# Layer 3's softmax sums gathered by accumulating DMAs in a four-layer graph network, with layer 0's residual by DMA and a new order

## The chip, the core and the metric

The kernel runs on one core of a Trainium2 chip. The time is that of one execution on the device, in microseconds (us), given as the median of several runs. A profile is a record of one such execution, with each instruction's start and length on each engine: PE (matrix products), PEld (its weight loads), DVE (vector), ACT (scalar), POOL (general, also a DMA issuer) and SP (a DMA issuer). Sixteen DMA engines move data for all issuers.

## The reference

Sixteen graphs of 1024 nodes with 128 features go through four layers. Each layer's result is added to its input and normalised over the features. `adj` holds zeros and ones; about one in 32 is one.

```python
# layer 0: one head of 128; attention over the neighbours
e = leaky_relu(s[:, :, None] + t[:, None, :], 0.2)
H_out = relu(softmax(e + mask) @ H)
# layer 1: 8 heads of 16, the same form, then elu
# layer 2: mean over the neighbours, times a matrix, plus a linear part; layernorm, relu
# layer 3: 4 heads of 32
Wh = einsum('bsf,hfd->bhsd', x, W)
scores = einsum('bhsd,bhtd->bhst', Wh, Wh) / sqrt(32)
scores = where(adj > 0, scores, NEG_INF)
h = einsum('bhst,bhtd->bhsd', softmax(scores), Wh)
# after every layer: x = layernorm(x + layer(x))
```

## The kernel before

The nodes of a graph are eight blocks of 128 (NB), in two halves of four blocks or 512 columns (HALF). The mask is loaded once per graph, transposed, as eight tiles m of 128 x 1024 in one-byte floats: POOL issues these DMAs (L557), and they turn integers into floats on the way. The softmax weights are always held transposed: a block of 128 source nodes on the partitions, the target nodes along the free axis.

**Layers 0 and 1.** DVE makes a tile of weights in one instruction (L636 in layer 0, L788 in layer 1): the larger of a row R, spread over all partitions, and a number per partition q, times the mask. PE multiplies it with the features (L648, L796). The row R is computed as a small column tile, turned by PE, copied by ACT, stored to memory by SP and read back by SP spread over all partitions (L753, 512 KB each); eight such rows are needed per graph in layer 1, four per group of heads. The factors that go into q and R come after a maximum over all partitions, an instruction on POOL (L398). Layer 0's result is taken from the accumulator by ACT with a relu (L669), which also sums it, and DVE adds the layer's input x0 (L689), which SP loaded in its natural form (L624).

**Layer 2** is a block of 96 products per half on the mask itself (L928), between turning x (L366), a product with the weights (L375) and a layernorm.

**Layer 3** is worked by halves of the target nodes and, in each half, by the eight source blocks j. ACT makes `gap` from the mask (L1066). PE first puts a large negative number where an edge is missing (L1076), then adds the scores (L1087), for four heads, into two PSUM tiles `sc` of two banks each from the pool `wk`. ACT takes the exponential of each (L1123) into a tile z3 of two heads. PE then multiplies (L1102): for each of two pairs of heads a step with four products, two heads times (their features, and a tile of ones). The features' products give the numerator and those with ones the sum of the weights, 32 equal rows of it. So a block j takes two such steps, and two accumulators (`acc3`) hold both pairs. At a half's end ACT copies the accumulators (L1139), PE turns them, and DVE divides (L1150, L1153) and adds to x3 (L1164).

**The order of the work.** All steps are handed to a planner that runs while the program is built. Each step has an engine, an estimated time, a due time, the buffers that it reads and writes and a lag until its result can be used. The planner goes through time and gives each engine the step that can start earliest, the one with the earlier due time first. The program is then one fixed order of instructions on every engine and each waits, in that order, for what it needs. Two or more graphs are in work at a time: layer 1 of one beside layers 2 and 3 of the one before. `PERIOD` is the distance between the due times of graphs. Buffers come from pools of fixed size: `wk` two tiles of two banks, `acc1` and `acc3` two banks each, z3 four tiles, R seven, z nine. Everything that is turned by PE (L366, L480) also goes through `wk`, as do the products before each layer.

Of the kernel before, what the change touches and what calls it, by code (L numbers as in the profile page):

```python
# [20 lines left out]
F32 = mybir.dt.float32  # L21
# [7 lines left out]
P = 128  # L29
# [47 lines left out]
class Plan:  # L77
# [8 lines left out]
    SAME = 0.0  # L86
    URGENT = 61.2
    AHEAD = 4322.0
# [136 lines left out]
def tile_binary(  # L225
# [3 lines left out]
    xT_in: bass.AP,  # L229
    adjT: bass.AP,  # L230
# [35 lines left out]
    acc3s = [psum.tile([P, HALF], F32, name=f"acc3_{n}") for n in range(2)]  # L266
# [25 lines left out]
    LATER1 = -3.8  # L292
    LATER3 = 48.7
# [28 lines left out]
    plan.scarce = ("wk", "acc1", "acc3")  # L322
    plan.pool("wk", wks)
    plan.pool("acc1", acc1s)
    plan.pool("acc3", acc3s)
    places("m", 6 * HB, [P, N], F8)
    places("R", 7, [P, N])
    places("z", 9, [P, N])
    places("z3", 4, [P, 2, HALF])
    places("oT1", 1, [P, N])  # L330
    places("oT3", 1, [P, N])
    places("x0", 1, [P, NB, P])
# [53 lines left out]
    def turned(x_nat, chunk, due):  # L386

        pt, xT = Buf("wk", "pt"), Buf("xTc", "xTc")
        step(
            "PE", 0.44, due, lambda: transposes(pt.t, [x_nat.t[:, chunk * HB + k, :] for k in range(HB)]),  # L390
            [(x_nat, chunk), xT], [pt],
        )
        step("ACT", 0.47, due, lambda: nc.scalar.copy(xT.t, pt.t[:, :HALF]), [pt], [xT])
        return xT
# [80 lines left out]
    def rows_everywhere(r, flat, count, due):  # L475

        pt, rT = Buf("wk", "pt"), Buf("rT", "rT")
        kept = Buf(f"rows{int(count > 1)}", "rows")
        step(
            "PE", 0.2, due, lambda: nc.tensor.transpose(pt.t[: count * NB, :P], flat(r.t), ident), [r, rT], [pt]  # L480
        )
        step("ACT", 0.2, due, lambda: nc.scalar.copy(rT.t[: count * NB, :], pt.t[: count * NB, :P]), [pt], [rT])
        step(
            "SP", 0.5, due,
            lambda: nc.sync.dma_start(
                out=kept.t.rearrange("h (k p) -> (h k) p", p=P), in_=rT.t[: count * NB, :]
            ),
            [rT], [kept], lag=2.5,
        )
        return kept  # L490
# [60 lines left out]
    def before0(b, due):  # L551
        G = graphs[b]
        G["m"] = [Buf("m", f"m_{b}_{j}") for j in range(NB)]
        for j, m in enumerate(G["m"]):
            step(
                "POOL", 0.55, due - 60 + 5 * j,
                lambda m=m, j=j: nc.gpsimd.dma_start(out=m.t, in_=adjT[b, j * P : (j + 1) * P, :]),  # L557
                [], [m], lag=5.0, floor=12.0 + 3 * j if b == 1 else max(due - 60 + 5 * j, 0.0),
            )
        x0 = G["x"] = Buf("x0", f"x0_{b}")  # L560
# [63 lines left out]
        step("SP", 2.0, due, lambda: nc.sync.dma_start(out=x0.t, in_=natural(x[b])), [], [x0], lag=2.5)  # L624

    def layer0(b, due):
# [4 lines left out]
        for half in range(2):  # L631
# [32 lines left out]
            for n in range(2):  # L664
# [23 lines left out]
                "DVE", 0.6, at,  # L688
                lambda ks=ks: nc.vector.tensor_tensor(y.t[:, ks, :], y.t[:, ks, :], G["x"].t[:, ks, :], ALU.add),  # L689
                [G["x"]], [(y, half)],  # L690
# [87 lines left out]
    def layer1(b, due, span):  # L778
# [3 lines left out]
        for g in range(2):  # L782
# [39 lines left out]
            oT, pt, rd = Buf("oT1", "oT1"), Buf("wk", "pb1"), little("rd1", [P, NB, G1, 1])  # L822
# [31 lines left out]
    def last1(b, due):  # L854

        G = graphs[b]
        o, x1, e = G["x2"], G["x1"], Buf("oT1", "e")
        step(
            "ACT", 1.0, due, lambda: nc.scalar.activation(e.t, o.t.rearrange("p k f -> p (k f)"), AF.Exp), [o], [e]
        )  # L860
        step(
            "DVE", 1.26, due,
            lambda: nc.vector.scalar_tensor_tensor(o.t, in0=o.t, scalar=0.0, in1=x1.t, op0=ALU.max, op1=ALU.add),
            [x1], [o],
        )
        step(
            "DVE", 1.26, due,
            lambda: nc.vector.scalar_tensor_tensor(o.t, in0=blocks(e.t), scalar=1.0, in1=o.t, op0=ALU.min, op1=ALU.add),
            [e], [o],
        )  # L870
        tot = little("tot", [P, NB])
        for half in range(2):
            sums(o, half, tot, due)
        layernorm(o, tot, due + 3)
# [114 lines left out]
    def before3(b, due):  # L989
# [6 lines left out]
        for chunk in range(2):  # L996
            xT, ps = turned(x3, chunk, due + chunk), Buf("wk", "h3")
# [18 lines left out]
            pt = Buf("wk", "pt")  # L1016
# [14 lines left out]
        sq, norms, bound = Buf("oT3", "sq"), little("norms", [P, NB * H3]), little("bound", [P, 1])  # L1031
# [23 lines left out]
    def layer3(b, due, span):  # L1055
# [3 lines left out]
        for half in range(2):  # L1059
            cols = slice(half * HALF, (half + 1) * HALF)  # L1060
            av = [Buf("acc3", f"av3_{g}") for g in range(2)]
# [34 lines left out]
            def weighted(j, g, z, av=av):  # L1096

                for h in range(2):
                    at = D3 * (2 * g + h)
                    for n, lhsT in enumerate((hhs[j // HB].t[:, j % HB, at : at + D3], ones)):  # L1100
                        at = 64 * h + 32 * n
                        nc.tensor.matmul(  # L1102
                            av[g].t[at : at + 32, :],
                            lhsT=lhsT,
                            rhs=z.t[:, h, :],
                            start=j == 0,
                            stop=j == NB - 1,
                        )

            for j in range(NB):  # L1110
# [4 lines left out]
                step("ACT", 0.68, at - 8, lambda j=j, gap=gap, f=missing: f(j, gap), [m[j]], [gap])  # L1115
# [12 lines left out]
                for g in (0, 1):  # L1128
                    step(
                        "PE", 0.87, at + LATER3, lambda j=j, g=g, z=zs[g], f=weighted: f(j, g, z),  # L1130
                        [zs[g], hhs[j // HB]], [av[g]], mode="32 columns",
                    )
            at = due + span * (half + 1) / 2
            oT, pt, rd = Buf("oT3", "oT3"), Buf("wk", "pb3"), little("rd3", [P, 2 * HB, 2, 1])
            o = Buf("rest", "o3")
            for g in range(2):
                step(
                    "ACT", 0.48, at,
                    lambda g=g, oT=oT, av=av: nc.scalar.copy(oT.t[:, g * HALF : (g + 1) * HALF], av[g].t),  # L1139
                    [av[g]], [(oT, g)],  # L1140
# [7 lines left out]
            def share(pt=pt, rd=rd, o=o):  # L1148
                pn = blocks(pt.t).rearrange("p m (c w) -> p m c w", c=2)
                nc.vector.reciprocal(rd.t, pn[:, :, :, D3 : D3 + 1])  # L1150
                for g in range(2):
                    of_g = slice(g * HB, (g + 1) * HB)
                    nc.vector.tensor_tensor(  # L1153
                        o.t.rearrange("p k (h d) -> p k h d", h=H3)[:, :, 2 * g : 2 * g + 2, :],
                        pn[:, of_g, :, :D3],
                        rd.t[:, of_g].to_broadcast([P, HB, 2, D3]),
                        ALU.mult,
                    )

            step("DVE", 1.07, at, share, [pt], [rd, o])  # L1160
# [22 lines left out]
    PERIOD = 129.0  # L1183
    weights(-198)
    for b in range(B):
        at = b * PERIOD
        at0 = 25 if b == 1 else at
        before0(b, at0 - 50)
        layer0(b, at0)
        before1(b, at + 25)  # L1190
        layer1(b, at + 99, 111)
        last1(b, at + 165)
        layer2(b, at + 165)
        before3(b, at + 223)
        layer3(b, at + 321, 108)
# [579 lines left out]
def tile_adj_resnorm(ctx: ExitStack, tc: tile.TileContext, x, adjT, *weights_and_out, xT):  # L1775
# [3 lines left out]
    tile_binary(tc, x, xT, adjT, *weights_and_out, wrong)  # L1779
# [44 lines left out]
```

## Time and profile before

| | |
|---|---|
| time, median of 3 runs | 2258.46 us (2258.31 to 2259.9) |
| the profiled execution, span from first to last instruction | 2254.1 us |
| PE busy | 2074.9 us, 92% of the span |
| DVE busy | 1902.1 us, 84% |
| ACT busy | 1743.5 us, 77% |
| POOL busy | 130.9 us, 6% |
| DMA moved | 119.86 MB, mean 53 GB/s |
| mean granted PE clock | 0.980 |

The profile gives no other time for the profiled execution than its span; the median of the runs lies 4.4 us above it. A line of a group names the line of the code, the engine, the operation, what it writes and reads, how often, then the time it was busy and the mean of one instruction in ns, and last how long its engine was idle just before and for whom it waited. In the 40 slices of the span each digit is a busy share in tenths. A busy PE isn't PE at its peak.

### The profile page before, as it was taken

How to read it: one execution, taken by the hardware profiler on the slowest of the kernel's cores; microseconds unless marked ns; L12 is line 12 of the kernel's file. 1: busy time of each engine (PE TensorE's matmuls, PEld its weight loads, DVE VectorE, ACT ScalarE, POOL GpSimd, SP SyncE). 2: the span in 40 equal slices, each digit the busy share in tenths (PEclk: the TensorE clock that was granted, in tenths of full speed). 3: DMA queues.
4: the chain of work that ended last, by engine and by line, in shares of the span. 5: the costliest groups of instructions: out<-in, count | busy, mean ns of one | idle time of the engine just before them, and what ended most of it. 6: DMA issues, size and time to landing. Idle time of an engine off the chain costs nothing.

```text
span 2254.1 us, 55458 instructions
## 1 busy us (share of the span) xinstructions
PE 2074.9 (92%) x23472; PEld 971.1 (43%) x23472; DVE 1902.1 (84%) x2854; ACT 1743.5 (77%) x4376; POOL 130.9 (6%) x187
## 2 busy tenths in 40 slices
PE   4857999999999999999999999999999999998876
PEld 4613545353534544363544535353454436242311
DVE  2899999989989989999999998998999999997211
ACT  3413769878787879878787987878787987868786
POOL 1010000100000000000000010000000000000000
PEclk9878999999999999999999999999999999999999
DMA  6122130312323040222314031232304122200000
GB/s 97 59 77 36 37 85 18 92 38 77 48 86 48 20 100 25 86 39 86 48 32 99 18 91 38 77 48 85 50 20 96 29 77 39 77 11 11 2 11 12
DMA packets 80851, 119.86 MB, mean 53 GB/s; under 512 B 7384, under 2 KB 58704, under 8 KB 80592
## 3 DMA queue, kind: packets, MB, share of 16 engines
q1 hardware_dynamic: 62160, 99.43, 13.1%
q0 software_dynamic: 18432, 16.79, 9.0%
q8 instruction: 186, 3.05, 0.6%
q14 instruction: 73, 0.60, 0.1%
HBM read 157.55 MB, written 8.97 MB: 74 GB/s over the span
## 4 chain that ended last, share of the span: by engine, by line
PE 52%; DVE 24%; ACT 20%; issue 3%; DMA 1%; POOL 0%; DVEq 0%; POOLq 0%; ACTq 0%
DVE z L788 18%; PE acc L648 10%; PE acc L1102 9%; PE acc L796 9%; PE wk L928 8%; ACT z L1123 6%; PE wk L1087 6%; PE wk L366 4%; ACT junk L430 4%; ACT x L468 3%; PE wk L375 3%; ACT gap L1066 3%; PE wk L1076 2%; PE wk L1001 1%; ACT hd L620 1%
## 5 line engine op out<-in xcount | busy, mean ns | idle before, releaser
L788 DVE SCALAR_TENSOR_TENSOR z<-R,q,m 128x1024 f32<-128x1024 f32 x1024 | 1248.9, 1279 | 16.1 <-PE acc L796 8.3
L1123 ACT ACTIVATE z<-wk,low 128x1024 f32<-128x1024 f32 x512 | 545.3, 1105 | 58.2 <-PE wk L1087 56.7
L796 PE MATMUL acc<-z,hh 128*32 128x512 f32 x4096 | 512.3, 612 | 46.1 <-DVE z L788 44.6
L1102 PE MATMUL acc<-z,hh 128*32 128x512 f32 x2048 | 516.2, 604 | 33.4 <-ACT z L1123 33.4
L1102 PE MATMUL acc<-z,ones 128*32 128x512 f32 x2048 | 516.1, 604 | 0.0
L430 ACT ACTIVATE junk<-x,off 128x128 f32<-128x128 f32 x640 | 256.2, 400 | 230.8 <-DVE off L424 214.6
L1087 PE MATMUL wk<-whT,turn 32*64 32x512 f32 x4096 | 286.3, 615 | 0.0
L468 ACT ACTIVATE x<-x,shift,rstd 128x128 f32<-128x128 f32 x640 | 259.3, 485 | 7.7 <-DVE shift L462 7.6
L648 PEld LDWEIGHTS acc<-hd,z 128*128 128x128 f32 x2048 | 237.3, 193 | 34.8 <-ACT x L669 12.6
L796 PEld LDWEIGHTS acc<-z,hh 128*32 128x32 f32 x4096 | 110.6, 110 | 326.8 <-issue 194.6
L648 PE MATMUL acc<-hd,z 128*128 128x129 f32 x2048 | 244.7, 278 | 5.9 <-DVE z L636 4.5
L1102 PEld LDWEIGHTS acc<-z,hh 128*32 128x32 f32 x2048 | 97.9, 109 | 279.1 <-issue 190.2
L928 PE MATMUL wk<-y,m 128*128 128x128 bf16 (+1 forms) x3072 | 182.9, 220 | 24.5 <-ACT z L1123 19.9
L1066 ACT ACTIVATE gap<-m,neg_one 128x512 bf16<-128x512 fp8e5 x256 | 183.4, 718 | 20.6 <-DMA m<-in_adj_dram 20.6
L928 PEld LDWEIGHTS <-m 128*128 128x128 fp8e5 x3072 | 181.0, 98 | 37.0 <-issue 27.3
L636 DVE SCALAR_TENSOR_TENSOR z<-R,q,m 128x512 f32<-128x512 f32 x240 | 162.8, 746 | 1.0 <-DMA R<-rows 1.0
L1102 PEld LDWEIGHTS acc<-z,ones 128*32 128x32 f32 x2048 | 97.6, 109 | 83.0 <-issue 83.0
L1076 PEld LDWEIGHTS <-far 32*32 32x32 bf16 x4096 | 35.7, 88 | 210.0 <-issue 198.2
L430 ACT ACTIVATION_READ_ACCUMULATOR junk<-x,off 128x1 f32 x640 | 120.4, 188 | 0.0
L1076 PE MATMUL wk<-gap,far 32*32 32x512 bf16 x4096 | 113.3, 386 | 3.4 <-DVE rest L1153 1.7
L557 POOL DMA_DIRECT2D m<-in_adj_dram x128 | 68.3, 540 | 796.2 <-ACT gap L1066 765.8
L1087 PEld LDWEIGHTS wk<-whT,turn 32*64 32x64 f32 x4096 | 59.8, 130 | 58.6 <-issue 58.6
(119 smaller groups left out, 1859.7 us busy)
## 6 DMA issues: line engine op xcount, KB each, us to landing
R<-rows SPq DMA_DIRECT2D x139, 512.0 KB
m<-in_adj_dram POOLq DMA_DIRECT2D x128, 128.0 KB, 5.6
xT<-in_xT_dram SPq DMA_DIRECT2D x32, 256.0 KB
x<-in_x_dram SPq DMA_DIRECT2D x16, 512.0 KB
out_dram<-x SPq DMA_DIRECT2D x15, 512.0 KB
rows<-rT SPq DMA_DIRECT2D x16, 32.0 KB
out_dram<-x SPq DMA_DIRECT2D x2, 256.0 KB
z<-in_L_gnn_a_dram SPq DMA_DIRECT2D x2, 128.0 KB
```

Source lines behind the costliest of these rows:

```text
L430: nc.scalar.activation(junk.t, y.t[:, k, :], AF.Square, bias=off.t[:, k : k + 1], accum_out=squared.t[:, k : k + 1])
L468: nc.scalar.activation(y.t[:, k, :], y.t[:, k, :], AF.Identity, bias=shift.t[:, k : k + 1], scale=rstd.t[:, k : k + 1])
L636: nc.vector.scalar_tensor_tensor(z.t[:, (j % 2) * HALF : (j % 2 + 1) * HALF], in0=R0.t[:, cols], scalar=q.t[:, j : j + 1], in1=m[j].t[:, c ...
L648: nc.tensor.matmul(av[k // 2].t.rearrange("p (k c) -> p k c", k=2)[:, k % 2, : P + 1], lhsT=z.t[:, at : at + P], rhs=hd.t[:, j, : P + 1], ...
L788: nc.vector.scalar_tensor_tensor(z.t, in0=G["R"][h].t, scalar=q.t[:, j, h : h + 1], in1=m[j].t, op0=ALU.max, op1=ALU.mult)
L796: nc.tensor.matmul(av[half].t[32 * c : 32 * c + 32, :], lhsT=hh.t[:, j, at : at + 32], rhs=zs[c].t[:, half * HALF : (half + 1) * HALF], st ...
L928: nc.tensor.matmul(ps.t[:, k * SLOT : k * SLOT + part.stop - part.start], lhsT=m[j].t[:, rows_i], rhs=y2.t[:, j, part], start=j == 0 and n ...
L1066: nc.scalar.activation(gap.t, m[j].t[:, cols], AF.Square, bias=neg_one, accum_out=squares[:, at : at + 1], saturate=False)
L1076: nc.tensor.matmul(sc[h // 2].t[c * 32 : (c + 1) * 32, (h % 2) * HALF : (h % 2 + 1) * HALF], lhsT=far[rows_r, rows_r], rhs=gap.t[rows_r, : ...
L1087: nc.tensor.matmul(sc[h // 2].t[r * 64 : (r + 1) * 64, (h % 2) * HALF : (h % 2 + 1) * HALF], lhsT=turns[j // HB].t[rows_h, j % HB * P + r ...
L1102: nc.tensor.matmul(av[g].t[at : at + 32, :], lhsT=lhsT, rhs=z.t[:, h, :], start=j == 0, stop=j == NB - 1,)
L1123: lambda g=g, sc=sc, zs=zs: nc.scalar.activation(zs[g].t.rearrange("p h n -> p (h n)"), sc[g].t, AF.Exp, bias=low.t, scale=S3),
```

## The change

In layer 3 the products with the tile of ones are no longer made for each block. A block's step on PE is now one set of four products, one for each head, into a single accumulator `av`. The exponentials of a half are added up in memory: the z3 tiles of the first block stay in place, and for each of the seven later blocks POOL issues two DMAs, one for each z3 tile, that add the tile (512 KB) onto that of the first block. When the last has landed, one set of four products with ones gives the sums of the weights for all four heads, into a bank of the new pool `one`. The planner counts 0.55 us for the issue of such a DMA and a lag of 5.0 (`SUMMED`).

In layer 0, DVE's addition of the input is replaced by two DMAs per graph, issued on POOL, that add x (given a second time by the host as `x_rows`, laid out by partition) onto y. The load of x0 on SP and its tile go.

Of the accumulators `acc3` one bank becomes the pool `one`, through which turned rows and layer 3's products before the scores now go in place of `wk`. z3 has six tiles in place of four; the three tiles oT1, oT3 and the two uses beside them share one tile `wide`. Due times, spacings and the planner's constants are new, so the order of the instructions on all engines is another.

```diff
-    SAME = 0.0
-    URGENT = 61.2
-    AHEAD = 4322.0
+    SAME = 0
+    URGENT = 63.35
+    AHEAD = 4322
...
-    acc3s = [psum.tile([P, HALF], F32, name=f"acc3_{n}") for n in range(2)]
+    acc3s = [psum.tile([P, HALF], F32, name="acc3_0")]
+    ones_psum = [psum.tile([P, HALF], F32, name="one_0")]
...
-    LATER1 = -3.8
-    LATER3 = 48.7
+    LATER1 = -5.84
+    LATER3 = 75.02
+    SUMMED = 5.0
...
-    places("z3", 4, [P, 2, HALF])
-    places("oT1", 1, [P, N])
-    places("oT3", 1, [P, N])
-    places("x0", 1, [P, NB, P])
+    places("z3", 6, [P, 2, HALF])
+    places("wide", 1, [P, N])
...
-        pt, xT = Buf("wk", "pt"), Buf("xTc", "xTc")
+        pt, xT = Buf("one", "pt"), Buf("xTc", "xTc")
...
-        pt, rT = Buf("wk", "pt"), Buf("rT", "rT")
+        pt, rT = Buf("one", "pt"), Buf("rT", "rT")
...
-        step("SP", 2.0, due, lambda: nc.sync.dma_start(out=x0.t, in_=natural(x[b])), [], [x0], lag=2.5)
...
             step(
-                "DVE", 0.6, at,
-                lambda ks=ks: nc.vector.tensor_tensor(y.t[:, ks, :], y.t[:, ks, :], G["x"].t[:, ks, :], ALU.add),
-                [G["x"]], [(y, half)],
+                "POOL", 0.55, at,
+                lambda ks=ks: nc.gpsimd.dma_start(out=y.t[:, ks, :], in_=x_rows[b, :, ks, :], accum_op=ALU.add),
+                [], [(y, half)], lag=SUMMED,
             )
...
-            xT, ps = turned(x3, chunk, due + chunk), Buf("wk", "h3")
+            xT, ps = turned(x3, chunk, due + chunk), Buf("one", "h3")
...
-            av = [Buf("acc3", f"av3_{g}") for g in range(2)]
+            av, weights_sum = Buf("acc3", "av3"), Buf("one", "sum3")
...
+            def weighted(j, zs, av=av):
+
+                for h in range(H3):
+                    nc.tensor.matmul(
+                        av.t[32 * h : 32 * h + 32, :],
+                        lhsT=hhs[j // HB].t[:, j % HB, h * D3 : (h + 1) * D3],
+                        rhs=zs[h // 2].t[:, h % 2, :],
+                        start=j == 0,
+                        stop=j == NB - 1,
+                    )
+
+            def totals(zs, into):
+
+                for h in range(H3):
+                    nc.tensor.matmul(
+                        into.t[32 * h : 32 * h + 32, :], lhsT=ones, rhs=zs[h // 2].t[:, h % 2, :], start=True, stop=True
+                    )
+
+            def added(z, into):
+                nc.gpsimd.dma_start(out=into.t, in_=z.t, accum_op=ALU.add)
...
-                for g in (0, 1):
+                step(
+                    "PE", 0.87, at + LATER3, lambda j=j, zs=zs, f=weighted: f(j, zs),
+                    [*zs, hhs[j // HB]], [av], mode="32 columns",
+                )
+                first = first or zs
+                for g in (0, 1) if j else ():
                     step(
-                        "PE", 0.87, at + LATER3, lambda j=j, g=g, z=zs[g], f=weighted: f(j, g, z),
-                        [zs[g], hhs[j // HB]], [av[g]], mode="32 columns",
+                        "POOL", 0.55, at + LATER3, lambda z=zs[g], into=first[g], f=added: f(z, into),
+                        [zs[g]], [first[g]], lag=SUMMED,
                     )
+            step(
+                "PE", 0.87, at + LATER3, lambda zs=first, into=weights_sum, f=totals: f(zs, into),
+                first, [weights_sum], mode="32 columns",
+            )
...
-    PERIOD = 129.0
-    weights(-198)
+    PERIOD = 123.89
+    weights(-160.44)
     for b in range(B):
         at = b * PERIOD
         at0 = 25 if b == 1 else at
-        before0(b, at0 - 50)
+        before0(b, at0 - 48.02)
         layer0(b, at0)
-        before1(b, at + 25)
-        layer1(b, at + 99, 111)
-        last1(b, at + 165)
-        layer2(b, at + 165)
-        before3(b, at + 223)
-        layer3(b, at + 321, 108)
+        before1(b, at + 9.06)
+        layer1(b, at + 95.36, 120.08)
+        last1(b, at + 154.67)
+        layer2(b, at + 147.85)
+        before3(b, at + 211.97)
+        layer3(b, at + 309.2, 104.17)
```

## The prediction

> **What bounds the kernel now.** I read first the page's busy shares and its 40 slices, then the steady stretch by windows, the chain, the groups, and last the DMA views.
>
> ```profile
> PE 2074.9 (92%) x23472; PEld 971.1 (43%) x23472; DVE 1902.1 (84%) x2854; ACT 1743.5 (77%) x4376; POOL 130.9 (6%) x187
> ...
> PE   4857999999999999999999999999999999998876
> ...
> DVE  2899999989989989999999998998999999997211
> ...
> DMA  6122130312323040222314031232304122200000
> ```
>
> PE and DVE are both near 9 tenths from slice 8 to slice 36, and the DMA engines at 2 to 3. So the share over the span hides a close race. The chain repeats itself: layer 2's block of products comes every 128.8 us (1220.11 - 1091.33, 1348.89 - 1220.11, and so on from 318.20 to 1864.22). Windows cut at these points give one period, one graph's worth of work:
>
> ```profile
> 446.99:575.79 128.80, 126.29 (x1462) 59.42 (x1462) 118.46 (x178) 108.17 (x274) 8.36 (x11) 1.00 0.24 59
> 1220.11:1348.89 128.78, 126.27 (x1462) 59.42 (x1462) 118.55 (x178) 108.16 (x274) 8.36 (x11) 1.00 0.26 59
> ```
>
> The columns are length, then busy PE, PEld, DVE, ACT, POOL, the granted clock, the DMA share, GB/s. PE works 126.3 of 128.8 us at clock 1.00: PE is the bound. DVE works 118.5 and idles 10.3, ACT 108.2, the DMA engines 0.25 x 128.8 = 32 us. The chain's PE stretches show the price of a weighting step of layer 3: 24 products in 2.58 us, so eight in 0.86.
>
> ```profile
> 1220.11 11.30 PE wk L928 x192
> ...
> 1284.93 2.58 PE acc L1102 x24
> ...
> 1348.89 11.30 PE wk L928 x192
> ```
>
> ```profile
> L1102 PE MATMUL acc<-z,hh 128*32 128x512 f32 x2048 | 516.2, 604 | 33.4 <-ACT z L1123 33.4
> L1102 PE MATMUL acc<-z,ones 128*32 128x512 f32 x2048 | 516.1, 604 | 0.0
> L1153 DVE TENSOR_TENSOR rest<-wk,rd 128x256 f32<-128x256 f32 x64 | 24.2, 420 | 1.1
> L689 DVE TENSOR_TENSOR x<-x,x 128x512 f32<-128x512 f32 x32 | 21.9, 683 | 1.1 <-ACT x L669 1.1
> ```
>
> **The change, part by part.**
>
> PE: 4096 instructions at L1102 over 16 graphs are 32 steps of eight per graph, 27.5 us. After it, each of 16 blocks needs one step, and each half one more for the sums: 18 x 0.86 = 15.5. PE falls by 12.0 to 114.3 us a graph.
>
> DVE: the residual add leaves (2 x 0.68), and the share of a half becomes one reciprocal and one product of 512 elements (0.26 + 0.69, the PSUM product at L845 lasting 0.69) for 0.26 + 0.76: 2 x 0.07. DVE falls by 1.5 to 117.0, and becomes the engine with most to do. ACT keeps its 108.2. If DVE idled as little as PE does now (2.5), the period would be 119.5. The order is written for graphs 123.89 apart (129.0 before, which ran as 128.8), so I take 123.9 for an order whose times are met.
>
> The gather: per half seven adds for each of two chains, 28 a graph, 512 KB each, SBUF to SBUF, all issued on POOL. Each waits for its exponential and for the landing of the add before it. The trace has no such DMA; the nearest is the load of m, also on POOL's queue, which reads 512 KB and writes 128.
>
> ```profile
> 1091.00:1098.00 7.00, 6.67 (x115) 6.67 (x115) 7.00 (x7) 2.69 (x6) 1.16 (x3) 1.00 1.06 96
> 1183.00:1191.00 8.00, 7.51 (x104) 1.47 (x96) 7.34 (x14) 7.72 (x23) 0.00 (x0) 1.00 1.00 379
> ...
> m<-in_adj_dram POOLq DMA_DIRECT2D x1, 128.0 KB, 3.8
> ...
> DMA to landing us min/median/max: 3.6/5.6/11.3
> ```
>
> With the engines full, m's arrive at 96 GB/s written, four times that read (384), and rows R at 379: 512 KB read takes 1.37 us whatever is written. A lone m lands in 3.8, so 2.4 is fixed. Here a rule weighs against the change: the Trainium skill ("Collectives: The Full Stack", section "The bandwidth ceiling: the fold count and why AG ≠ RS ≠ AR") says that a DMA that adds reads two sources through one ring and so delivers half a copy's rate. By the row alone (one read) a gather add lands in 3.8, all of them hold the engines 28 x 1.37 = 38 us a graph, and nothing is late. By the rule it is 2.75 us of engine time, 5.2 to landing when alone, and 77 us a graph. I take the rule for the size, since two operands do have to be read, and the row for the rate; no run here shows it yet. The floor is 1.37, and no row gives a ceiling.
>
> Engine time is then 77 + 32 = 109 us of 123.9, or 88%, from 25%. The order counts 0.55 + 5.0 = 5.55 us for each add, alone. Two adds of a pair share the ring, so the second lands at about 5.2 + 2.75 = 7.9 after the first's issue, and a pair needs 5.5: the chain can hold 5.55 a block while nothing else moves, but not more.
>
> Beside the rows R it can't. Today R's seven transfers fill the engines from 1181 to 1191, in the very stretch where layer 3 runs fastest, one block in 4 us:
>
> ```profile
> 1186.12 2.12 ACT L1123 ACTIVATE z<-wk,low 128x1024 f32<-128x1024 f32 x2
> 1189.92 2.10 ACT L1123 ACTIVATE z<-wk,low 128x1024 f32<-128x1024 f32 x2
> 1194.04 2.10 ACT L1123 ACTIVATE z<-wk,low 128x1024 f32<-128x1024 f32 x2
> 1198.00 2.10 ACT L1123 ACTIVATE z<-wk,low 128x1024 f32<-128x1024 f32 x2
> ```
>
> There R (10.3 us alone) and the adds stretch each other to some 20 us. R's fourth row, due at 5.5 us of engine time, comes up to 5.5 later; some 4 of these lie beside the layernorm work that DVE had between 1184 and 1190, which leaves 1.5 a graph. The adds fall behind by up to 10: 20 / 5.5 = 3.6 pairs due, half of it done. What is late next is the third-next exponential (z3 has three pairs, one held for the whole half), with 5.55 - 2.2 = 3.3 us to spare; then ACT, and PE behind it. DVE can write nine z ahead, 9 x 1.28 = 11.5 us, and PE has 9.6 us spare a graph, so I let this hide the rest (6.6 us if the cover were gone). Taken: 123.9 + 1.5 = 125.4.
>
> POOL's queue is in order. The two residual adds (256 KB each, two reads, 1.37 of engine time, 3.8 to landing) wait for ACT's shares; behind them stand gathers, m loads and the three all-reduces of a graph. The second share ends at 1143.2 and the squares that read y start at 1147.96: 4.8 us cover 3.8, by ACT's copies of turned heads (L1012, L1014); without these 3.8 a graph. The layernorm's offset reads only the sums, so doesn't wait. An all-reduce behind a waiting add stands up to 5.5, and with it DVE's L733 or low; the order places these with the 5.0 counted, and their lateness is that of the gather. SP loses 16 loads of x (0.4 us each, on a queue that mostly waits); the adds move as many bytes.
>
> The bank for turned rows: transposes waited for exponentials to free wk, PE idle 8.2 us in 5 such waits at L366 and 5.5 in 14 at L480, so at most 0.9 a graph; one bank now serves six uses in a row before layer 3, so I take 0. Likewise 0 for the shared wide tile (held some 2 us at a time) and for the sums' wait at each half's end inside the steady stretch, hidden by PE's other graph; uncovered it is 5.5 twice a graph.
>
> The end has no cover. The last graph's exponentials run from 2172.87, and its products end at 2238.8: 66 us, PE-bound at 3.77 a block. After the change the chain sets it: 5.9 us to the second block, 7 x 5.55, 2.2, 7 x 5.55, 0.9 for the sums = 87. That is +21 (+13 at 5.0 a pair); I take +22 with the extra half-end.
>
> **Sum.** Fourteen of the intervals between layer 2's blocks are full (twelve of 128.8, one of 122.8, one of 130.4; the last, 113.1, has no next graph). Span: 2254.1 - 14 x (128.8 - 125.4) + 22 = 2228.5. The median of the runs, 2258.46, lies 4.4 over the span; so 2233. Of PE's 12.0 us a graph DVE's floor leaves 9.3, the order's spacing 4.9, R's lateness 3.4, and the end takes 22 / 14 = 1.6 of these back.
>
> **Rivals.**
>
> *The gather comes late and the order breaks (slower).* The place is the stretch around R's arrival; the price is the 6.6 us a graph above, if ACT's and PE's delay isn't hidden because DVE waits there for R and for all-reduces standing behind late adds on POOL. Period 130.5: 2254.1 + 14 x 1.7 + 22 + 4.4 = 2304. It decides once the period is over 128.8 - 22 / 14 = 127.2, that is 1.8 beyond what I took. For it: 88% of DMA time against lags counted as if alone. Against it: the mean need is 123.9 / 16 = 7.7 us a block, and the nine z. 2263 to 2400.
>
> *An add takes far longer than two reads.* Fourteen in a row per graph plus 8 us of half-ends exceed 128.8 from 8.6 us each. At 10: 148 a graph, and the end 14 x 10 + 9 - 66 = 83 longer: 2254.1 + 14 x 19.2 + 83 + 4.4 = 2610. Nothing in the trace speaks for it except that no add is there.
>
> *DVE's floor is reached:* period 119.5 to 122, 2150 to 2185. The DMA share speaks against it.
>
> *No change:* period near 127.2; gain and tail cancel.
>
> **How the numbers follow.** Likeliest, the order held but for R: 2195 to 2254, 0.40, time 2233. DVE's floor (below 2195): 0.10. No change, 2254 to 2263: 0.06 (0.2% is about what a measurement of this kernel tells from nothing). Late gather: 0.34. Far slower, over 2400: 0.10. Faster 0.50, same 0.06, slower 0.44. The range 2168 to 2400 leaves out half of the floor's and all of the far slower case.
>
> **What would show it.** Right: layer 3's products of z at 2304 instructions in place of 4096; PE near 114 of some 125 us a period and DVE near 117; the DMA share at 0.8 or more; the adds landing in 5 to 8 us; R late by a few; 80 to 90 us for the last graph's exponentials. Wrong: ACT or PE idle for landings of z, all-reduces that stand behind adds while DVE is idle, a period over 127; or adds that land in under 4 us (one read, period 123.9, 2212) or over 9.

## The result, and the profile after

The changed kernel takes 2461.02 us (median of 4 runs, 2458.08 to 2465.26) against 2259.18 (2258.31 to 2261.74): a ratio of 1.0892, 95% interval 1.0874 to 1.0911. It is 9% slower; 2233 was forecast.

From its page, the busy shares, four of the rows of 40 slices, the two DMA queues that matter and four of the groups:

```profile
span 2463.5 us, 53104 instructions
...
PE 2028.2 (82%) x21680; PEld 945.8 (38%) x21680; DVE 1885.2 (77%) x2790; ACT 1749.9 (71%) x4376; POOL 533.3 (22%) x667
...
PE   4857889797988979797989979798898979897775
...
DVE  2898798788878888888889878888888888884201
...
PEclk8878989898999989898999989999999989898876
DMA  6130666968788787968778797878768696866586
...
q0 software_dynamic: 87552, 260.09, 60.9%
q1 hardware_dynamic: 45520, 91.04, 11.0%
...
L788 DVE SCALAR_TENSOR_TENSOR z<-R,q,m 128x1024 f32<-128x1024 f32 x1024 | 1255.3, 1279 | 157.9 <-DMA R<-rows 133.4
...
L1115 POOL DMA_DIRECT2D z<-z x448 | 381.8, 863 | 1316.4 <-ACT z L1131 566.6
...
L1099 PE MATMUL acc<-z,hh 128*32 128x512 f32 x2048 | 288.2, 635 | 10.6 <-ACT z L1131 10.6
...
L636 DVE SCALAR_TENSOR_TENSOR z<-R,q,m 128x512 f32<-128x512 f32 x240 | 165.6, 746 | 69.3 <-DMA m<-in_adj_dram 69.3
```

PE and DVE do less work than before and neither stays at 9 tenths. The DMA row went from 2 or 3 tenths to 7 or 8. DVE's two lines that make weights (L788, L636) now show idle time in front of them, for the rows R and for the masks m. These are not the tiles that the new DMAs move.

Layer 2's block of products now comes every 140.2 us in place of 128.8 (484.9 to 1325.9 in six periods). Windows over these six periods and over one (columns as in the prediction), and over a stretch of the last graph's exponentials:

```profile
484.90:1325.90 841.00, 726.91 (x8103) 343.92 (x8102) 698.65 (x1034) 649.52 (x1638) 199.79 (x246) 0.95 0.79 158
1048.90:1189.45 140.55, 120.09 (x1353) 56.89 (x1351) 117.28 (x174) 108.29 (x273) 33.10 (x41) 0.95 0.80 158
2343.00:2383.00 40.00, 29.53 (x336) 7.13 (x336) 5.05 (x14) 32.53 (x65) 10.78 (x15) 0.84 0.90 171
```

DVE works 116.4 us of 140.2 and idles 23.7; before it was 118.5 and 10.3. What it waited for over these six periods, in us in total, times, and the longest:

```profile
DVE z L788 <- DMA R<-rows: 59.3, 21, 7.2
DVE z L636 <- DMA m<-in_adj_dram: 34.2, 6, 6.1
DVE degrees L945 <- PE wk L928: 21.5, 7, 6.4
DVE z L788 <- PE acc L796: 9.0, 6, 1.5
```

Per graph that is 9.9 us for R and 5.7 for m. The same view of the kernel before, over seven periods (445.4 to 1347.3), has no wait for m, and for R this:

```profile
DVE z L788 <- DMA R<-rows: 1.2, 2, 1.0
```

PE, which still has the longer busy time (121.2 us a graph), waits behind DVE. Of its 19.0 us of idle time a graph 15.7 are waits for DVE's z; before it was 0.1. ACT waits 4.9 us a graph for adds, but little of that reaches PE: its waits for ACT are 3.0 a graph, after 2.4. From the views of PE and ACT over the six periods:

```profile
PE acc L796 <- DVE z L788: 83.7, 23, 10.7
PE acc L648 <- DVE z L636: 10.4, 6, 2.1
```

```profile
ACT z L1131 <- DMA z<-z: 29.4, 6, 6.5
```

Two places in the timeline show how it happens. First the last mask of a graph, which POOL issues at 1074.01 behind four adds since 1065.21. DVE is ready for it 1.6 us later and waits 5.13:

```profile
1065.21 1.86 POOL L1115 DMA_DIRECT2D z<-z  x2 [16.32 <-ACT z L1131]
...
1073.47 0.84 POOL L1115 DMA_DIRECT2D z<-z  x1 [1.65 <-ACT gap L1066]
1074.01 0.87 POOL L559 DMA_DIRECT2D m<-in_adj_dram  x1
...
1074.86 0.74 DVE L636 SCALAR_TENSOR_TENSOR z<-R,q,m 128x512 f32<-128x512 f32 x1
...
1080.74 1.41 DVE L636 SCALAR_TENSOR_TENSOR z<-R,q,m 128x512 f32<-128x512 f32 x2 [5.13 <-DMA m<-in_adj_dram]
```

The chain of waits goes through both places:

```profile
1065.21 8.80 DMA z<-z x3
1074.01 6.71 DMA m<-in_adj_dram
...
1138.62 14.37 DMA R<-rows
```

Then the rows R. SP stores their source (32 KB, L487) and issues seven loads when it has landed, here 6.07 us later, while adds are in flight. DVE waits for R three times, and ACT for an add (SP's and DVE's parts of the timeline):

```profile
1129.97 0.46 SPq L487 DMA_DIRECT2D rows<-rT  x1
1136.04 5.80 SPq L753 DMA_DIRECT2D R<-rows  x7
```

```profile
1143.64 2.48 DVE L788 SCALAR_TENSOR_TENSOR z<-R,q,m 128x1024 f32<-128x1024 f32 x2 [7.23 <-DMA R<-rows]
...
1149.06 1.11 ACT L1131 ACTIVATE z<-wk,low 128x1024 f32<-128x1024 f32 x1 [6.52 <-DMA z<-z]
1149.19 1.28 DVE L788 SCALAR_TENSOR_TENSOR z<-R,q,m 128x1024 f32<-128x1024 f32 x1 [1.61 <-DMA R<-rows]
...
1153.08 1.28 DVE L788 SCALAR_TENSOR_TENSOR z<-R,q,m 128x1024 f32<-128x1024 f32 x1 [2.60 <-DMA R<-rows]
```

In this stretch the DMA share is 1.02: the sixteen engines are full.

```profile
1136.00:1153.00 17.00, 6.92 (x88) 2.12 (x80) 5.64 (x8) 9.50 (x26) 2.89 (x4) 0.83 1.02 261
```

### The profile page after: what moved, and what is told of

It reads as the page before. It is cut to its first block, busy times and chain, and to the rows that moved or that the text cites. A ratio compares the mean times of both kernels' runs of the same rounds, so it can differ in the third digit from the quotient of the medians.

```text
span 2463.5 us, 53104 instructions
## 1 busy us (share of the span) xinstructions
PE 2028.2 (82%) x21680; PEld 945.8 (38%) x21680; DVE 1885.2 (77%) x2790; ACT 1749.9 (71%) x4376; POOL 533.3 (22%) x667
## 4 chain that ended last, share of the span: by engine, by line
DVE 26%; DMA 24%; PE 23%; issue 14%; ACT 11%; POOL 2%; SPq 1%; POOLq 0%; DVEq 0%; ACTq 0%
DVE z L788 18%; DMA z<-z 13%; DMA R<-rows 6%; PE acc L796 6%; DMA m<-in_adj_dram 4%; PE acc L648 4%; ACT z L1131 3%; PE wk L928 3%; ACT x L470 3%; PE wk L1087 2%; PE wk L377 2%; PE acc L1099 2%; ACT junk L432 2%; PE one L368 1%; POOL all L400 1%
## 5 line engine op out<-in xcount | busy, mean ns | idle before, releaser
L788 DVE SCALAR_TENSOR_TENSOR z<-R,q,m 128x1024 f32<-128x1024 f32 x1024 | 1255.3, 1279 | 157.9 <-DMA R<-rows 133.4
L796 PE MATMUL acc<-z,hh 128*32 128x512 f32 x4096 | 556.5, 653 | 214.4 <-DVE z L788 212.7
L1115 POOL DMA_DIRECT2D z<-z x448 | 381.8, 863 | 1316.4 <-ACT z L1131 566.6
L1087 PE MATMUL wk<-whT,turn 32*64 32x512 f32 x4096 | 304.4, 652 | 0.0
L796 PEld LDWEIGHTS acc<-z,hh 128*32 128x32 f32 x4096 | 108.1, 113 | 510.4 <-DVE z L788 299.0
L1099 PE MATMUL acc<-z,hh 128*32 128x512 f32 x2048 | 288.2, 635 | 10.6 <-ACT z L1131 10.6
L648 PE MATMUL acc<-hd,z 128*128 128x129 f32 x2048 | 257.9, 281 | 28.7 <-DVE z L636 24.5
L648 PEld LDWEIGHTS acc<-hd,z 128*128 128x128 f32 x2048 | 245.0, 195 | 70.4 <-DVE z L636 34.5
L1076 PE MATMUL wk<-gap,far 32*32 32x512 bf16 x4096 | 151.1, 403 | 86.6 <-ACT z L1131 77.8
L636 DVE SCALAR_TENSOR_TENSOR z<-R,q,m 128x512 f32<-128x512 f32 x240 | 165.6, 746 | 69.3 <-DMA m<-in_adj_dram 69.3
L1076 PEld LDWEIGHTS <-far 32*32 32x32 bf16 x4096 | 46.3, 88 | 314.1 <-issue 309.0
L1099 PEld LDWEIGHTS acc<-z,hh 128*32 128x32 f32 x2048 | 49.9, 111 | 188.5 <-issue 165.6
L559 POOL DMA_DIRECT2D m<-in_adj_dram x128 | 79.9, 661 | 75.9 <-ACT gap L1066 73.4
L689 POOL DMA_DIRECT2D x<-in_x_rows_dram x32 | 27.4, 856 | 306.0 <-ACT x L669 306.0
```

The lines of the kernel that those rows point to most:

```text
L648: nc.tensor.matmul(av[k // 2].t.rearrange("p (k c) -> p k c", k=2)[:, k % 2, : P + 1], lhsT=z.t[:, at : at + P], rhs=hd.t[:, j, : P + 1], ...
L788: nc.vector.scalar_tensor_tensor(z.t, in0=G["R"][h].t, scalar=q.t[:, j, h : h + 1], in1=m[j].t, op0=ALU.max, op1=ALU.mult)
L796: nc.tensor.matmul(av[half].t[32 * c : 32 * c + 32, :], lhsT=hh.t[:, j, at : at + 32], rhs=zs[c].t[:, half * HALF : (half + 1) * HALF], st ...
L1076: nc.tensor.matmul(sc[h // 2].t[c * 32 : (c + 1) * 32, (h % 2) * HALF : (h % 2 + 1) * HALF], lhsT=far[rows_r, rows_r], rhs=gap.t[rows_r, : ...
L1087: nc.tensor.matmul(sc[h // 2].t[r * 64 : (r + 1) * 64, (h % 2) * HALF : (h % 2 + 1) * HALF], lhsT=turns[j // HB].t[rows_h, j % HB * P + r ...
L1099: nc.tensor.matmul(av.t[32 * h : 32 * h + 32, :], lhsT=hhs[j // HB].t[:, j % HB, h * D3 : (h + 1) * D3], rhs=zs[h // 2].t[:, h % 2, :], st ...
```

## The experiments

**Adds of a sixteenth of the size.** Everything of the changed kernel stays (order, waits, number of DMAs), but each add moves 32 KB in place of 512.

```diff
-                nc.gpsimd.dma_start(out=into.t, in_=z.t, accum_op=ALU.add)
+                nc.gpsimd.dma_start(out=into.t[:, 0, :64], in_=z.t[:, 0, :64], accum_op=ALU.add)
...
-                 nc.vector.reciprocal(rd.t, pn[:, HB:, :, :1])
+                 nc.vector.tensor_scalar(rd.t, pn[:, HB:, :, :1], 0.0, 1e-6, ALU.mult, ALU.add)
```

> The changed kernel with its order, its waits and the number of its adds as they are, but each gather add moves only 64 of a tile's 1024 columns, and the reciprocal of the sums is a constant (so the sums are left out, and DVE keeps an instruction of that size). Engine time for the adds falls from 28 x 2.75 = 77 us a graph to under 8, and they land in 3 to 4 us, under the 5.55 that the order counts. Theory A (the adds hold the 16 engines, so that R, m and the next adds come late): the period falls from 140 to 124 or 125, the waits of DVE for R and m mostly go, the time is 2200 to 2230. Theory B (the place of things in POOL's queue: m, all-reduces and residuals stand behind adds that wait for exponentials, at any size of the adds): DVE still waits about 5 us a graph for m, and the time stays over 2350. Theory C (the order itself is bad, whatever the adds cost): over 2430.

Measured: 2251.42 us (2250.95 to 2256.1), a ratio to the kernel before of 0.9971 (0.9956 to 0.9986). The period is 126.9. Windows over seven periods, and two lines from the view of waits and the one of DMAs:

```profile
455.20:1343.70 888.50, 831.58 (x9454) 398.15 (x9451) 818.31 (x1212) 755.80 (x1912) 244.51 (x287) 0.98 0.35 67
```

```profile
DVE z L636 <- DMA m<-in_adj_dram: 9.1, 7, 1.9
```

```profile
z<-z POOLq DMA_DIRECT2D x448, 32.0 KB, 2.2
```

So 210 us of the changed kernel (2461 - 2251) are the size of the adds. The order, POOL's issues and the waits for the adds' completion were all still there. Theories B and C are out: DVE waits 1.3 us a graph for m, not 5. Theory A fits, but its range was missed by 21 us, as the period is 126.9 and not 124 or 125. The run also shows how little this order had to gain: with adds of a sliver it is 0.3% faster than the kernel before. Even these hold the engines 11 us a graph (next experiment), and no run is without them.

**Copies in place of adds.** The same 512 KB, but the destination isn't read.

```diff
-                nc.gpsimd.dma_start(out=into.t, in_=z.t, accum_op=ALU.add)
+                nc.gpsimd.dma_start(out=into.t, in_=z.t)
...
-                 nc.vector.reciprocal(rd.t, pn[:, HB:, :, :1])
+                 nc.vector.tensor_scalar(rd.t, pn[:, HB:, :, :1], 0.0, 1e-6, ALU.mult, ALU.add)
```

> The changed kernel with each gather add made a plain copy of the same 512 KB between the same tiles (the sums are left out, and the reciprocal is a constant). If an add costs two reads, engine time falls from 77 to 38 us a graph, the DMA share from 0.80 to about 0.55, the landing from 6.0 to about 4.5, which is under the order's 5.55; theory A then gives a period of 124 to 129 and 2200 to 2290. If the addition's second read cost nothing on the engines, share and time stay as they are, near 2460. Theory B: over 2350, as the queue is the same.

Measured: 2316.28 us (2314.52 to 2318.04), ratio 1.0248 (1.0228 to 1.0269), period 131.6. The queue's line of the page, windows over seven periods, and DVE's waits in them:

```profile
q0 software_dynamic: 87552, 260.09, 36.9%
```

```profile
465.20:1386.50 921.30, 839.69 (x9454) 398.12 (x9451) 819.82 (x1212) 757.95 (x1912) 175.06 (x287) 0.97 0.54 169
```

```profile
DVE z L788 <- DMA R<-rows: 29.6, 24, 3.7
...
DVE z L636 <- DMA m<-in_adj_dram: 15.7, 7, 3.1
```

The share (0.54) is what two reads against one would give, and a copy lands in 3.7 us. The time lies between theory A's range (to 2290) and B's (from 2350), so the expectation was missed by 26 us: waits for R and m remain, 4.2 and 2.2 a graph.

The queue's share gives the price of one. Its other loads (m and x) take 11.5% of a span of 2255.0 us = 259 in the last kernel below, which has no such adds; they are taken to be the same here. Then an add is (0.609 x 2463.5 - 259) / 448 = 2.77 us on sixteen engines, a copy (0.369 x 2312.7 - 259) / 448 = 1.33, and the thin add (0.195 x 2249.2 - 259) / 448 = 0.40. Per graph, 28 of them are 78, 37 and 11 us, and the period is 140.2, 131.6 and 126.9: about 0.2 us of period for each us of DMA time, from the thin add to the copy (4.7 for 26) as from the copy to the add (8.6 for 41). A copy also takes POOL less time to issue (530 ns for 848), but that isn't what costs: a thin add takes as long to issue as a whole one (852).

**Thin rows R.** The changed kernel, but SP loads only the first eighth of each row R in layer 1; the tiles are filled with ones at the start.

```diff
-    places("R", 7, [P, N])
+    for t in places("R", 7, [P, N]):
+        nc.vector.memset(t, 1.0)
...
-                lambda h=h, R=R: nc.sync.dma_start(out=R.t, in_=kept.t[h, :].partition_broadcast(P)),
+                lambda h=h, R=R: nc.sync.dma_start(out=R.t[:, :P], in_=kept.t[h, :P].partition_broadcast(P)),
```

> The changed kernel with its adds whole, but each of layer 1's rows R loaded over 128 of its 1024 columns (the rest keeps ones or old numbers, so layer 1's weights are not the reference's; seven fills of R are added at the start, 5 to 7 us). R's engine time falls from some 11 to 1.4 us a graph. Theory A, in the form that the loss is DVE's wait for R (9.9 us a graph) and for m (5.7): DVE's wait for R falls under 2, the wait for m stays near 5, the period goes from 140.1 to 130 to 132 and the time to 2310 to 2350. Rival (the chain of adds with its z3 tiles sets the period, and R only waits where there is room): R's wait goes, but ACT's and PE's waits for z take its place and the time stays over 2420.

Measured: 2368.97 us (2366.21 to 2371.73), ratio 1.0488 (1.0467 to 1.0509), period 134.2. So 92 us of the loss go with R's bytes. The expectation was missed by some 20 us, since DVE's wait for R fell from 9.9 to 3.5 a graph and no further: an eighth of a row still takes 5.0 us to land. The wait for m is as it was. The rival is out: ACT's waits for adds didn't take R's place, but fell from 4.9 to 1.1 a graph.

```profile
R<-rows SPq DMA_DIRECT2D x124, 64.0 KB, 5.0
```

```profile
DVE z L637 <- DMA m<-in_adj_dram: 40.5, 7, 6.6
...
DVE z L789 <- DMA R<-rows: 24.2, 12, 3.8
```

**Thin rows and thin masks.** On top of it, masks are loaded by their first eighth from the fourth graph on.

```diff
-                lambda m=m, j=j: nc.gpsimd.dma_start(out=m.t, in_=adjT[b, j * P : (j + 1) * P, :]),
+                lambda m=m, j=j, w=N if b < 3 else P: nc.gpsimd.dma_start(out=m.t[:, :w], in_=adjT[b, j * P : (j + 1) * P, :w]),
```

> The changed kernel with thin rows R (first 128 of 1024 columns) and, from the fourth graph on, thin mask loads too (first 128 of 1024 columns; the rest keeps an earlier graph's mask). Most of R and of the masks is left out, so the output is another. The adds are whole. If what costs is the total time on the DMA engines, taking the masks' 7/8 of 11 us a graph away acts like taking R away did (5.9 us of period for some 8 x 1.2 us): the wait for m falls from 5.8 a graph to under 3, the period from 134.2 to about 131, the time to 2315 to 2340. If instead small loads wait behind the adds whatever their own size, m's wait stays at 5 or more, R's at 3 or more, the period at 133 or more and the time at 2350 to 2370.

Measured: 2338.9 us (2335.54 to 2345.39), ratio 1.0346 (1.0329 to 1.0364), period 132.0 (592.68 to 1912.48 in ten). The time is inside the first theory's range, at its upper edge; the wait for m lies between the two: 3.9 a graph, with 16 KB still taking 4.6 us to land. Both have a part in it: the bytes of R and m, and a delay behind the adds that doesn't go away when the load itself is small.

```profile
DVE z L637 <- DMA m<-in_adj_dram: 39.1, 10, 4.4
DVE z L789 <- DMA R<-rows: 34.6, 16, 3.6
```

**Rows that don't wait for their store.** What remains of R's wait with thin rows, 3.5, is near to what the 32-KB store ahead of them lost: it lands in 1.8 us with thin adds, 5.6 in the changed kernel, 5.2 with thin R. Here R is loaded from another array, so nothing waits for the store; once with whole rows and once with thin ones (the latter with `[b, h, :P]` into `R.t[:, :P]`, from the kernel with thin R).

```diff
-                lambda h=h, R=R: nc.sync.dma_start(out=R.t, in_=kept.t[h, :].partition_broadcast(P)),
+                lambda h=h, R=R: nc.sync.dma_start(out=R.t, in_=xT_in[b, h, :].partition_broadcast(P)),
```

> The changed kernel with layer 1's rows R loaded from another array of the same shape (a row of 1024 numbers of the transposed input), so that they don't wait until the small store of the true row (32 KB, by SP) has landed; R holds other numbers, so the output is another. That store lands in 5.6 us in the changed kernel and in 1.8 with thin adds. If it is a link in R's lateness, R's loads start some 5 us earlier, DVE's wait for R falls from 9.9 a graph to 4 to 6, the period from 140.2 to 135 to 137 and the time to 2380 to 2420. If R is late only because the engines are full of its own bytes and the adds, an earlier start meets the same full engines: the wait stays at 8 or more and the time at 2435 or more.

> The same on top of the thin rows R (first 128 of 1024 columns, so most of R is left out as well). There DVE still waited 3.5 us a graph for R, and the store landed in 5.2 in place of the 1.8 with thin adds. If those 3.4 us are the store's, the wait falls under 1, the period from 134.2 to 131 to 132.5, the time from 2369 to 2325 to 2350. If they are the thin loads' own delay behind the adds, the wait stays at 2.5 or more and the time at 2355 to 2370.

Measured with whole rows: 2454.12 us (2449.73 to 2456.05), ratio 1.0863 (1.0844 to 1.0883), period 139.0 (571.23 to 1543.93 in seven). With thin ones: 2354.37 (2351.13 to 2356.17), ratio 1.0422 (1.0405 to 1.0439), period 131.7 (551.71 to 1473.55). DVE's waits for R, whole and thin:

```profile
DVE z L788 <- DMA R<-in_xT_dram: 47.6, 21, 3.1
```

```profile
DVE z L789 <- DMA R<-in_xT_dram: 2.2, 3, 0.9
```

With thin rows the store is nearly the whole of the remaining wait, 3.5 down to 0.3, though the time gains 15 us and not the 19 or more expected. With whole rows the loads start some 5 us earlier and meet the same full engines: their median landing grows from 9.1 to 10.1, DVE's wait goes from 9.9 to 6.8, ACT's for adds grows from 4.9 to 7.1 a graph (below), and 7 us of time are gained. The time is the second theory's, the wait lies between the two.

```profile
ACT z L1131 <- DMA z<-z: 50.0, 21, 4.1
```

**An order that counts what was measured.** The changed kernel with the add's lag at 6.5 and its issue at 0.85, R's steps on SP at 2.5 with a lag of 4.0, and due times chosen anew with these.

```diff
-    SUMMED = 5.0
+    SUMMED = 6.5
...
-                "SP", 1.7, due + 60 * (h // G1) + h,
+                "SP", 2.5, due + 60 * (h // G1) + h,
...
-                    [kept], [R], lag=2.0,
+                    [kept], [R], lag=4.0,
...
-    PERIOD = 123.89
+    PERIOD = 122.77
```

> The changed kernel's steps in an order made with lags nearer to what was measured: 0.85 us for an add's issue and 6.5 to landing (instead of 0.55 and 5.0), 2.5 us a row and a lag of 4.0 for R (instead of 1.7 and 2.0), and due numbers fitted to these. If the order's false lags were the cause: under 2310. Theory A (the engines are 80% taken by the adds whatever the order, and what comes in bursts comes late): 2310 to 2420, better than 2461 but slower than before. Theory B likewise loses part of its cost, as m and all-reduces are placed with true lags.

Measured: 2441.46 us (2437.86 to 2445.07), ratio 1.0802 (1.0779 to 1.0826), period 138.4, with the DMA share at 0.81. The expectation was missed: the order earns 20 us, not 40 to 150. DVE's wait for R falls to 2.5 a graph, but ACT now waits 7.1 for adds, and PE 11.5 for ACT (over seven periods). Here the first rival of the prediction, ACT and PE held up by the adds, does come about:

```profile
ACT z L1131 <- DMA z<-z: 49.6, 27, 3.5
```

```profile
PE wk L1076 <- ACT z L1131: 80.7, 43, 4.2
```

The store of R's source lands in 1.8 us in this order, where it took 5.6 in the changed kernel. It falls into a gap between adds: the DMA share is 0.07 while the store at 968.37 is under way. The one at 1129.97 in the changed kernel came just behind two adds, and the share until R's loads was 0.84.

```profile
rows<-rT SPq DMA_DIRECT2D x16, 32.0 KB, 1.8
```

```profile
968.37:970.19 1.82, 1.82 (x28) 0.42 (x16) 1.82 (x3) 0.93 (x1) 0.00 (x0) 1.00 0.07 18
```

So which transfer is late depends on the order. Some were late in both orders that were tried with all 28 adds.

**Gather by twos.** Block 2i+1 is added onto block 2i, and PE multiplies each such sum with ones: 16 adds a graph in place of 28, none waiting for another, and 24 steps on PE in place of 18. Turned rows go through `wk` again; due times are chosen anew.

```diff
-                first = first or zs
-                for g in (0, 1) if j else ():
+                if j % 2 == 0:
+                    first = zs
+                    continue
+                for g in (0, 1):
```

> The gather in a smaller dose: blocks are added by twos (16 adds a graph in place of 28, none waiting for an earlier add), and the products with ones are made once for two blocks (24 steps of eight in place of 18); turned rows go through wk again; lags of 0.85 and 6.0 and due numbers fitted to them. Engine time for adds 16 x 2.8 = 45 us a graph, DMA share about 0.55. Theory A: between the copies' 131.5 and the kernel before: 2270 to 2330. If a long chain of adds was the cause rather than engine time, there is no chain here: under 2258.

Measured: 2360.36 us (2360.27 to 2360.44), ratio 1.045 (1.0431 to 1.0469), period 135.0 at a DMA share of 0.58. The expectation was missed. DVE's waits for R are 1.9 a graph, and none is for m; the larger ones are for PE (3.3 in front of L843, 3.0 of L947, 2.6 of L790), which works 122.6, then 2.6 for ACT and 2.1 for the store of the output. This order has losses of its own, so the run doesn't tell whether the chain of adds costs anything beside their size. That stays open.

**Layer 0's residual alone.** The kernel before with only x added by DMA, once with its due times as they are and once with due times chosen anew.

```diff
-                "DVE", 0.6, at,
-                lambda ks=ks: nc.vector.tensor_tensor(y.t[:, ks, :], y.t[:, ks, :], G["x"].t[:, ks, :], ALU.add),
-                [G["x"]], [(y, half)],
+                "POOL", 0.55, at,
+                lambda ks=ks: nc.gpsimd.dma_start(out=y.t[:, ks, :], in_=x_rows[b, :, ks, :], accum_op=ALU.add),
+                [], [(y, half)], lag=5.0,
```

> The kernel before with layer 0's residual by DMA alone (and its due numbers as before, so the planner's order shifts a little). DVE gives up 1.4 us a graph but PE sets the period of 128.8; the two adds have 4.8 us of cover. Theories A and B: no change, 2252 to 2268. If residual adds on POOL were a cause of the loss by themselves (a wait of ACT's squares for their landing, 3.8 us a graph uncovered): 2290 to 2320.

> Layer 0's residual by DMA without the gather, with due numbers fitted to it. PE still has 126.3 us a graph and sets the period, so theory A leaves at most what PE idles (2.5 us a graph) and what the ends have: 2235 to 2260, faster than before by 0 to 1%. If the residual adds hurt by their place on POOL, 2260 or more as with the due numbers of before.

Measured: 2263.59 us (2259.65 to 2268.35), ratio 1.0021 (1.0014 to 1.0028), and 2256.13 (2252.97 to 2259.12), ratio 0.9988 (0.9982 to 0.9995), both as expected. DVE loses 1.5 us of work a graph, but PE, with 126.1 of 128.9 us, is still the bound. Of the kernels that compute the reference the second is the fastest one measured, ahead of the kernel before by a tenth of a per cent.

```profile
447.80:1349.80 902.00, 882.71 (x10239) 416.94 (x10234) 818.80 (x1226) 755.71 (x1912) 70.39 (x90) 1.00 0.26 59
```

## Why the prediction was wrong

DVE's time in a period is its work plus its waits. The same account for each kernel (us a graph, from windows and waits over six to ten periods):

| | period | DVE works | idle | for R | for m | for other things |
|---|---|---|---|---|---|---|
| before | 128.8 | 118.5 | 10.3 | 0.2 | 0 | 10.1 |
| predicted | 125.4 | 117.0 | 8.4 | 1.5 | 0 | 6.9 |
| thin adds | 126.9 | 116.9 | 10.0 | 0 | 1.3 | 8.7 |
| copies | 131.6 | 117.1 | 14.5 | 4.2 | 2.2 | 8.1 |
| thin R and m | 132.0 | 117.1 | 14.9 | 3.5 | 3.9 | 7.5 |
| thin R, no store | 131.7 | 117.2 | 14.5 | 0.3 | 5.5 | 8.7 |
| thin R | 134.2 | 116.4 | 17.9 | 3.5 | 5.8 | 8.6 |
| whole R, no store | 139.0 | 117.3 | 21.6 | 6.8 | 5.7 | 9.1 |
| changed | 140.2 | 116.4 | 23.7 | 9.9 | 5.7 | 8.1 |
| true lags | 138.4 | 117.3 | 21.1 | 2.5 | 4.3 | 14.3 |

In the seven kernels with the changed order (thin adds to changed) the last column stays between 7.5 and 9.1; nearly all of the difference in period stands in the columns for R and m. With the true lags much of it moves to the last column.

**The step that failed** is the one on the rows R: "R's fourth row ... comes up to 5.5 later", 1.5 a graph after DVE's other work, with the rest hidden by the nine z and PE's 9.6 us, and the masks, whose loads stand in the same queue as the adds, left at no cost. The mechanism was named, its size was off by ten times: 15.6 us a graph (9.9 and 5.7) in place of 1.5. Three things were wrong in it.
- It made lateness one event, R's fourth row. The store of R's source stands ahead of all seven loads and comes 3.8 us later (5.6 for 1.8); then R's own bytes share full engines. DVE waits three or four times a graph (21 times in six), the first time for up to 7.2. Thin rows take 6.4 us of this away, and taking the store away as well the other 3.2.
- The nine z can't cover it: they are what DVE writes. A stock of its output helps when others wait. Here DVE itself waits for its inputs, and PE waits behind it (15.7 us a graph): at those times no z stood ready, and time that PE has to spare doesn't bring DVE's inputs sooner.
- No line of the sum asked what becomes of the masks. In the trace of before, POOL issues a graph's last mask 10 us ahead of its use (984.22; DVE's weights from it begin at 994.28 or later). In the changed order DVE is ready for it 1.6 us after the issue, with thin adds 2.6. Thin adds make this a wait of 1.3, with the mask landing in 3.7; whole ones of 5.7, landing in 6.7. That the order had moved the mask to its need went unseen; that adds stretch the landing was not counted. What moving the masks' issue back alone would give was not tried.

In the sum this is 8.4 + 5.7 of the 14.8 us between 125.4 and 140.2; other waits give 1.2, and DVE's work takes 0.6 back. By the runs, the size of the adds costs 13.3 us a graph (140.2 - 126.9), where 1.5 was taken; and 123.9, the spacing that the order was written for, was not reached even with thin adds (126.9). Fourteen intervals of 14.8 are 207 of the 235 us by which the span is over the forecast's 2228.5. Of the others, 10 lie ahead of layer 2's first block (201.3 after 191.2; thin adds have 8 of them), 5 behind its last. About 6 are in the last interval, which has no next graph (117.7 after 111.7), and 6 in intervals longer than 140.2. The prediction read the first interval of before as 122.8; by the products' first starts it is 127.0 (191.2 to 318.2), which changes nothing in the sum.

**What was right.** DVE's work (117.0; 116.4). PE's products of z (2048 at L1099 and 256 for the sums, 2304). The price of an add: the rule that an adding DMA reads two sources, which the Trainium skill ("Collectives: The Full Stack", section "The bandwidth ceiling: the fold count and why AG ≠ RS ≠ AR") states for the reduce step of a ReduceScatter, gave 2.75 us; it took 2.77, with the copy at 1.33; the lone exponentials' window says the same, 171 GB/s at a share of 0.90, which is 190 at full share, half of the 379 of R. DMA time 109 us a graph: 0.80 x 140.2 = 112. Adds landing in 5 to 8: 6.0 in the median, 4.5 to 14.2. The end was near: +22 forecast, and 163.3 us behind layer 2's last block in place of 136.1, so +27 (but see below). The all-reduces: 0.3 us a graph of DVE's time, as before. The residual's adds at no cost: 1.0021 and 0.9988.

**What else was off.** PE works 121.2 us, not 114.3, and so stays the engine with the longest busy time. It does the products forecast (1350 a graph) at a granted clock of 0.95 in place of 1.00, a matmul of L1099 taking 635 ns in place of 604. Most of its idle time is a wait for DVE, so this should cost little; no run tests it. The last graph's exponentials were to take 80 to 90 us, 87 by the sum; from the first of them to the end of the sums it is 97:

```profile
2351.03 2.12 ACT L1131 ACTIVATE z<-wk,low 128x1024 f32<-128x1024 f32 x2
```

```profile
2445.94 1.92 PE L1110 MATMUL one<-z,ones 128*32 128x512 f32 x4 [1.14 <-DMA z<-z]
```

And "by the row alone ... nothing is late" fell as well: copies, with one read, leave DVE waiting 6.4 us a graph and take 2316 us in place of the 2212 given for them.

**The rivals.** "The gather comes late and the order breaks" had the place and the sign. Its price, 6.6 us a graph, was the unhidden lateness of ACT and PE, and ended at 2304; the measured 15.6 is DVE's own for R and m. The time fell in the range of "an add takes far longer", whose mechanism is refuted: an add took what was forecast. What the trace of before could have told: of DVE's 10.3 us of idle time a graph, 8.6 were waits for PE and ACT. Such waits stayed at 7.5 to 9.1 in the changed order, though PE had fewer products to make, and R's and m's came on top of them nearly whole. That idle time was no slack in which a late row or mask could hide.

## What to carry to other kernels

Work that was moved from a busy engine to the DMA engines was paid for here by other transfers in the same stretch. Before such a move, list the transfers that the engine with least slack waits for, and ask how late each becomes at the new share, small ones and those in series (a store, then its loads) too. Buffers of an engine's output hide nothing when its inputs are late. Before such a gather is tuned, run it with the adds cut to a sliver: here this gave about the gain that the order could have (0.3%) and the price of the adds' size (210 us) at once.

## What the runs showed of the hardware that was not expected

- An accumulating DMA takes POOL longer to issue: 848 ns in the median for one of 512 KB, 852 for one of 32 KB, 530 for the copy. At 28 a graph POOL is busy 33 us of 140 in place of 8.
- Its time on the engines isn't in proportion to its size: 0.40 us for 32 KB against 2.77 for 512.
- Small transfers beside the adds landed late in the changed order: 5.6 us for the 32-KB store (1.8 with thin adds, 2.7 with copies), 5.0 for 64 KB of R, 4.6 for 16 KB of m. This depends on what is under way at the time: with true lags, where the store at 968.37 fell into a gap between whole adds, its median is 1.8 again, and by twos too.
- PE's granted clock was 0.95 in the steady stretch with PE busy 86% of it, 0.98 with thin adds (94%), 1.00 before (98%). The busy share alone doesn't set it: at 91% it was 0.97 with copies and 0.99 in the gather by twos.
